# Layer 1's neighbour sums issued one slot at a time behind half products, and two blocks flipped through a diagonal

## The chip, the core and the metric

The kernel runs on one core of a Trainium2 chip. A core has five engines that each work through a queue of their own, in order: TensorE (PE, matrix products; its weight loads are listed as PEld), VectorE (DVE), ScalarE (ACT), GpSimd (POOL) and SyncE (SP). Transfers are issued from SP's and POOL's queues; the indirect ones, which gather or scatter rows by an index, all come from POOL. The metric is device time in microseconds (us) of one execution; lower is better.

## The reference

Two graph layers over 2708 nodes with 1024 features, all in float32. `adj` is a sparse 0/1 matrix; a few nodes have many neighbours, most have one to five, many none.

```python
def _L0_gnn_ref(sent_embed, adj_tensor, W_q, b_q, W_k, b_k, W_v, b_v):
    q, k, v = ...
    z = scale * (q @ k.T)
    spare_z = z * adj_tensor
    spare_z = jnp.where(spare_z == 0.0, -10000.0, spare_z)
    out = softmax(spare_z, axis=1) @ v
    return relu(out)
def _L1_gnn_ref(x, adj, weight, bias):
    return jnp.matmul(adj, jnp.matmul(x, weight)) + bias
x = _layernorm(x + _L0_gnn_ref(x, adj, ...))
x = _layernorm(x + _L1_gnn_ref(x, adj, ...))
```

Only layer 1 is touched by the change. Its result for one node is the normalised sum of the node's own row, the bias, and (sum of its neighbours' rows of x1) times the 1024x1024 weight, where x1 is layer 0's output.

## The kernel before

**Tiles.** The nodes are sorted by their number of neighbours into 22 blocks of up to 128 rows (P = 128). Block b has room for SLOTS[b] neighbours: 15, 11, 8, 6, 5, 4, 3 and 2 for blocks 0 to 7; 13, 5, 4, 4, 3, 3, 3, 2, 2, 2, 1 and 1 for blocks 8 to 19; blocks 20 and 21 have none. Blocks 18 and 19, which have one slot, are called `single`. The busiest rows are dealt out over several rows of block 0 and of a further block, "hub", with 11 slots and its sum in the tile `part`. `tabs` holds each row's neighbour indices, `valid` a 1 or 0 per slot. An index beyond the last row is left out by the gather, and `valid` then takes the slot's old contents out of the sum.

**Layer 1.** For each block, every slot is gathered from x1 in DRAM by an indirect transfer (`gather_slot`, line 483, POOL) into one of nine tiles named g, which are used in turn (`g_tile`), and added into the block's r by VectorE, times `valid` (line 1480). The first slot of most blocks is gathered straight into r; where not every row has a neighbour (block 0, hub, the single blocks and block 7), the first slot goes to a g tile and a pass of VectorE multiplies it by `valid` into r (line 1477). Then r is transposed ("flipped") on PE into rT: `flip` (line 953) makes eight transposes of 128x128 in two groups of four, ACT copies each group out of PSUM. Block 0's flip (`flip_shares`, line 966) is a matmul with a matrix of zeros and ones in the identity's place, which also folds in the hub's shares. Blocks are worked in pairs ("units"), in this order: (19, 18), (17, 16), (15, 1), (14, 2), (7, 8), (9, 3), (4, 10), (5, 11), (6, 0), (12, 13).

A unit's product is Strassen's scheme with seven half products (`pair_products`, line 311 through `half_products`), each of four matmuls of 128x128 by 128x512. It needs four sums of the halves of rT on VectorE (lines 1212 to 1215) and three differences of weight quarters besides a fourth made in place, t1 to t4 (lines 1537 to 1540, 128x2048 each), made once. Each half product's PSUM bank is emptied by one VectorE pass (line 333 or 1517, "eviction"), which has a high priority in the planner; several banks go on accumulating after an eviction, so a later half product of the unit waits for the eviction of an earlier one. The evictions add into xr, a gather of x1's own row onto a copy of the bias (line 467 on POOL, line 1490 on ACT). ACT normalises, POOL scatters the output rows (line 940).

**Order.** The program is emitted in the order of the Python code, and a planner moves instructions on each queue by priority and by when it thinks them ready. `follow(later, earlier)` adds a dependency; with same=True it only orders two instructions of the planner without a semaphore. In iteration i of the loop over units the sums of unit i+3 are emitted as a whole ahead of unit i's products; those of unit 2 stand in iteration 0, behind `halves_turned[-1]`, and the hub's in iteration 4. The list `began` holds the first matmul of every half product, and `between[n]` holds functions that are called while half product n is emitted, with its first matmul as argument; layer 0 uses it already.

**The seam.** Layer 0's last pair of blocks is normalised and scattered to x1 by a chain over VectorE (BN statistics line 1239, aggregate line 1019, four small passes), ACT and POOL; every gather of layer 1 waits for it. Meanwhile PE runs WARM = 13 matmuls whose result nobody reads (line 1530). The four quarters of the layer's weight are loaded by SP (line 1447) as soon as the last products on their buffers are done. The first difference t1 has a `follow` behind `firsts[0]`, the first mask pass of layer 1:

```python
follow(nc.vector.tensor_sub(t1, t1, w11), firsts[0], same=True)
nc.vector.tensor_sub(t2, w22, t1)
nc.vector.tensor_sub(t3, t2, w11)
nc.vector.tensor_sub(t4, w21, t2)
```

Of the kernel before, what the change touches and what calls it, by code (L numbers as in the profile page):

```python
# [9 lines left out]
F32 = mybir.dt.float32  # L10
# [6 lines left out]
ALU = mybir.AluOpType  # L17
# [4 lines left out]
P = 128  # L22
# [5 lines left out]
HUB_SLOTS = 11  # L28
HUB_KEYS = 80
RUN = 12  # L30
WARM = 13
FAMILY = 8


# [2 lines left out]
MIXED = [7]  # L37
# [7 lines left out]
RB = 5  # L45
# [39 lines left out]
def sparse_part(ctx, tc, x, xT, adj, wqT, wkT, wvT, bq, bk, bv, w1, b1, out):  # L85
    nc = tc.nc
    N, D = x.shape
# [11 lines left out]
    J0 = SLOTS[0]  # L99
    URGENT = 2000  # L100
    last = [b for b in range(NB) if SLOTS[b] == 0]
    single = [b for b in range(NB) if SLOTS[b] == 1]
# [11 lines left out]
    with es:  # L114
# [149 lines left out]
        def follow(later, earlier, same=False):  # L264

            kind = mybir.DependencyClass.NoSync if same else mybir.DependencyClass.Sync
            tc.add_manual_dep(later.ins, earlier.ins.name, mybir.DependencyInfo(kind, mybir.DependencyReason.DATA),
                              reason="an engine's queue shall not stand still for a transfer")
# [642 lines left out]
        def g_tile():  # L911

            filled[1] += 1
            return gp.tile([P, D], F32, name="g", tag=f"g{filled[1] % G1}", bufs=1)
# [31 lines left out]
        def flip(r, rT=None):  # L946

            rT = wp.tile([P, DC, P], F32, name="rT") if rT is None else rT
            for g in range(DC // 4):
                tr = p_tr.tile([P, 4, P], F32, name="tr")  # L950
                for k in range(4):
                    c = g * 4 + k
                    nc.tensor.transpose(tr[:, k, :], r[:, c * P:(c + 1) * P], ident)  # L953
                nc.scalar.copy(rT[:, g * 4:g * 4 + 4, :], tr)  # L954
            return rT

        def flip_shares(shares, rT=None):

            rT = wp.tile([P, DC, P], F32, name="rT") if rT is None else rT
            for g in range(DC // 4):  # L960
                tr = p_tr.tile([P, 4, P], F32, name="tr")
                for k in range(4):
                    c, at = g * 4 + k, 0
                    for r, to in shares:
                        n = to.shape[1]
                        nc.tensor.matmul(tr[:, k, at:at + n], r[:, c * P:(c + 1) * P], to, start=True, stop=True)
                        at += n
                nc.scalar.copy(rT[:, g * 4:g * 4 + 4, :], tr)
            return rT
# [231 lines left out]
        halves_turned = []  # L1201

        def turn_pair(flips, pool):

            A = []
            for k, flip_to in enumerate(flips):
                rT = pool.tile([P, DC, P], F32, name="rT", bufs=4)
                A.append(flip_to(rT))
            (a11, a12), (a21, a22) = [(a[:, :DC // 2], a[:, DC // 2:]) for a in A]
            s_all = wm_pool.tile([P, 4, DC // 2, P], F32, name="s_all", tag="m3")  # L1210
            S = [s_all[:, i] for i in range(4)]
            nc.vector.tensor_add(S[0], a21, a22)
            nc.vector.tensor_sub(S[1], S[0], a11)
            nc.vector.tensor_sub(S[2], a11, a21)
            halves_turned.append(nc.vector.tensor_sub(S[3], a12, S[1]))
            return A, S
# [243 lines left out]
        units = [(19, 18), (17, 16), (15, 1), (14, 2), (7, 8), (9, 3), (4, 10), (5, 11), (6, 0), (12, 13)]  # L1460
        assert sorted(last + [b for unit in units for b in unit]) == list(range(NB))
        last_norm = applied[-1]
        firsts = []

        def sum_rows(b, k=0, behind=None):
            if b == "hub":
                n, tab, ok, r = P, tab_h, valid_h, part
            else:
                n, tab, ok = (P, tab0, valid0) if b == 0 else (rows[b], tabs[:, b, :SLOTS[b]], valid[:, b, :SLOTS[b]])
                r = (cp if k else rp).tile([P, D], F32, name="r", bufs=3 if k else RB)  # L1470
            for j in range(tab.shape[1] if b else J0):
                if j == 0 and b not in [0, "hub"] + single + MIXED:
                    gather_slot(x1_d[:, :], tab[:n, 0:1], n, r)
                    continue
                xg = gather_slot(x1_d[:, :], tab[:n, j:j + 1], n, g_tile())
                if j == 0:
                    put = nc.vector.tensor_scalar(r[:n], xg[:n], ok[:n, 0:1], None, op0=ALU.mult)
                    firsts.append(put)
                else:
                    put = nc.vector.scalar_tensor_tensor(r[:n], xg[:n], ok[:n, j:j + 1], r[:n], op0=ALU.mult, op1=ALU.add)  # L1480
                if behind is not None:
                    follow(put, behind, same=True)
                    behind = None
            return r

        def gather_x1(b, k=0):

            n = rows[b]
            xr = (cp if k else wp).tile([P, D], F32, name="xr", bufs=2)
            follow(nc.scalar.copy(xr[:n], bias1[:n]), last_norm, same=True)  # L1490
            return gather_at(x1_d[:, :], tabs[:n, b, ROW:ROW + 1], n, xr, ALU.add)
# [12 lines left out]
            scatter(out, b, n, t, "out")  # L1504

        def turn1(unit, rs):
            return turn_pair([lambda rT, b=b, r=r: flip_shares([(part, to_h), (r, to_0)], rT) if b == 0 else flip(r, rT)
                              for b, r in zip(unit, rs)], cp)

        def work1(unit, A, S, xrs):  # L1510
# [20 lines left out]
            follow(put, products[-1], same=True)  # L1531

        got1, turned1, pending = {}, {}, []
        got1[0] = [sum_rows(b, k) for k, b in enumerate(units[0])]
        got1[1] = [sum_rows(b, k) for k, b in enumerate(units[1])]
        turned1[0] = turn1(units[0], got1.pop(0))
        follow(nc.vector.tensor_sub(t1, t1, w11), firsts[0], same=True)
        nc.vector.tensor_sub(t2, w22, t1)
        nc.vector.tensor_sub(t3, t2, w11)
        nc.vector.tensor_sub(t4, w21, t2)  # L1540
        xrs = {0: [gather_x1(b, k) for k, b in enumerate(units[0])]}
        for i, unit in enumerate(units):
            for p in pending:
                finish1(*p)
            if i + 1 < len(units):
                turned1[i + 1] = turn1(units[i + 1], got1.pop(i + 1))
                xrs[i + 1] = [gather_x1(b, k) for k, b in enumerate(units[i + 1])]
            if i == 0:
                got1[2] = [sum_rows(b, k, halves_turned[-1]) for k, b in enumerate(units[2])]
            if i + 3 < len(units):  # L1550
                got1[i + 3] = [sum_rows(b, k) for k, b in enumerate(units[i + 3])]
            if i == 4:
                sum_rows("hub")
            pending = list(zip(unit, *work1(unit, *turned1.pop(i), xrs.pop(i))))
            if i == len(units) - 4:
                some = test_scores()
            if i == len(units) - 2:
                raise_flag(some)
            if i in (4, 6):
                b = last[i // 2 - 2]  # L1560
                pending.append((b, gather_x1(b), None))
        for p in pending:
            finish1(*p)
        raised = nc.values_load(flag, min_val=0, max_val=1, skip_runtime_bounds_check_because="a comparison's result")
# [319 lines left out]
```

## Time and profile before

| | |
|---|---|
| median of 3 runs | 1009.27 us (1007.11, 1009.27, 1018.39) |
| the profiled execution | 1011.19 us, span 1009.5 us |
| PE busy over the span | 957.8 us (95%) |
| VectorE busy | 815.7 us (81%) |
| POOL busy (indirect transfers in layer 1) | 553.2 us (55%) |
| granted clock of TensorE, mean | 0.983 |
| layer 0's last half product ends | 697.24 us |
| first flip of layer 1 | 711.16 us |
| last half product of layer 1 ends | 995.83 us |

Times inside the execution are counted from the span's start. A line of the timeline gives the start, the length, the engine, the line of the kernel, the operation, what it writes and reads by the program's names, the shapes and the number of records; a matmul of 512 columns makes two records, a transpose one. In brackets stand the idle time of the engine ahead and what ended it. A busy PE isn't PE at full speed: the granted clock shows where the throttle had it slower.

### The profile page before, as it was taken

How to read it: one execution, taken by the hardware profiler on the slowest of the kernel's cores; microseconds unless marked ns; L12 is line 12 of the kernel's file. 1: busy time of each engine (PE TensorE's matmuls, PEld its weight loads, DVE VectorE, ACT ScalarE, POOL GpSimd, SP SyncE). 2: the span in 40 equal slices, each digit the busy share in tenths (PEclk: the TensorE clock that was granted, in tenths of full speed). 3: DMA queues.
4: the chain of work that ended last, by engine and by line, in shares of the span. 5: the costliest groups of instructions: out<-in, count | busy, mean ns of one | idle time of the engine just before them, and what ended most of it. 6: DMA issues, size and time to landing. Idle time of an engine off the chain costs nothing.

```text
span 1009.5 us, 10470 instructions
## 1 busy us (share of the span) xinstructions
PE 957.8 (95%) x2723; PEld 452.3 (45%) x2723; DVE 815.7 (81%) x1813; ACT 461.5 (46%) x1142; POOL 553.2 (55%) x443
## 2 busy tenths in 40 slices
PE   7989999999999999999899999999899899999994
PEld 6434444444444444454444444444444444435441
DVE  8999996995678896998899999984668977868532
ACT  4553466655543434233643544563242444252832
POOL 3841056133677574445466785621877878868420
PEclk9999999999999999999999999999999999989998
DMA  8475687769889676346537897756887699977631
GB/s 346 152 238 177 209 262 223 232 229 249 237 250 326 219 231 211 118 141 194 167 97 227 266 304 236 220 170 228 199 285 226 210 319 338 300 234 199 213 105 45
DMA packets 101342, 222.92 MB, mean 221 GB/s; under 512 B 19492, under 2 KB 46892, under 8 KB 101272
## 3 DMA queue, kind: packets, MB, share of 16 engines
q0 software_dynamic: 49424, 152.74, 49.8%
q1 hardware_dynamic: 51848, 69.41, 21.2%
q8 instruction: 23, 0.38, 0.1%
q14 instruction: 47, 0.39, 0.1%
HBM read 211.80 MB, written 33.64 MB: 243 GB/s over the span
## 4 chain that ended last, share of the span: by engine, by line
PE 52%; DVE 20%; issue 11%; DMA 7%; POOL 4%; ACT 4%; SPq 0%; POOLq 0%; DVEq 0%; ACTq 0%
PE po L311 29%; PE po L391 11%; PE tr L391 5%; PE tr L311 3%; DVE r L1097 3%; DVE junkv L1038 2%; DMA xr<-x_d,tabs 2%; DVE t L333 2%; DVE r L1480 2%; POOL wk_i L301 1%; POOL g L483 1%; DVE junkv L1294 1%; DVE at_a L242 1%; PE tr L953 1%; DMA g<-x_d,tabs 1%
## 5 line engine op out<-in xcount | busy, mean ns | idle before, releaser
L483 POOL DMA_INDIRECT g<-in_x_dram,tabs x84 | 112.6, 1341 | 81.9 <-DVE past_end L663 26.9
L311 PE MATMUL po<-t,s_all 128*128 128x512 f32 x320 | 146.2, 599 | 7.5 <-issue 3.8
L391 PE MATMUL po<-m,xt 128*128 128x512 f32 x288 | 124.8, 592 | 0.0
L1480 DVE SCALAR_TENSOR_TENSOR r<-g,valid,r 128x1024 f32<-128x1024 f32 x77 | 98.0, 1280 | 11.9 <-DMA g<-x_d,tabs 7.2
L311 PEld LDWEIGHTS po<-t,s_all 128*128 128x128 f32 x320 | 60.5, 191 | 85.8 <-issue 77.0
L483 POOL DMA_INDIRECT g<-x_d,tabs x66 | 77.4, 1172 | 26.0 <-issue 13.7
L1097 DVE SCALAR_TENSOR_TENSOR r<-g,pr,r 128x1024 f32<-128x1024 f32 x64 | 81.9, 1281 | 6.4 <-ACT r L1095 5.8
L1038 DVE SCALAR_TENSOR_TENSOR junkv<-yg,g 128x1024 uint8<-128x1024 f32 x69 | 84.4, 1224 | 2.6 <-DMA g<-in_x_dram,tabs 2.0
L391 PEld LDWEIGHTS po<-m,xt 128*128 128x128 f32 x288 | 54.6, 190 | 68.2 <-issue 67.4
L954 ACT COPY rT<-tr 128x512 f32<-128x512 f32 x76 | 41.6, 587 | 95.1 <-PE tr L953 93.5
L1000 ACT ACTIVATE junks<-t,lnm 128x1024 uint8<-128x1024 f32 (+1 forms) x40 | 45.8, 1144 | 84.6 <-DVE lnm L998 84.5
L242 DVE FIND_INDEX8 at_a<-ones,a 128x8 uint16<-128x234 f32 (+5 forms) x132 | 82.2, 627 | 0.0
L311 PE MATMUL po<-w,rT 128*128 128x512 f32 x160 | 75.2, 612 | 4.4 <-DVE t L1517 4.2
L256 ACT ACTIVATE junk<-a 128x2756 uint8<-128x2756 uint32 (+1 forms) x22 | 55.0, 2501 | 42.8 <-issue 15.8
L311 PE MATMUL po<-t,rT 128*128 128x512 f32 x160 | 73.7, 603 | 0.4 <-DVE t L1517 0.4
L311 PE MATMUL po<-wv,rT 128*128 128x512 f32 x160 | 73.5, 604 | 0.0
L311 PE MATMUL po<-w,s_all 128*128 128x512 f32 x160 | 73.4, 598 | 0.0
L311 PE MATMUL po<-wv,s_all 128*128 128x512 f32 x160 | 72.3, 592 | 0.0
L462 ACT ACTIVATE junka<-xt 128x128 f32<-128x128 f32 x168 | 51.7, 308 | 37.9 <-PE po L311 18.3
L1038 DVE SCALAR_TENSOR_TENSOR junkv<-xr,g 128x1024 uint8<-128x1024 f32 x37 | 45.4, 1226 | 19.1 <-DMA g<-in_x_dram,tabs 11.3
L940 POOL DMA_INDIRECT x_d<-t,tabs x22 | 27.7, 1257 | 51.3 <-ACT t L1014 17.6
L391 PE MATMUL tr<-m,xt 128*128 128x512 f32 x128 | 55.6, 592 | 0.0
(423 smaller groups left out, 1835.7 us busy)
## 6 DMA issues: line engine op xcount, KB each, us to landing
xt<-in_xT_dram SPq DMA_DIRECT2D x21, 512.0 KB
y_d<-yo SPq DMA_DIRECT2D x21, 512.0 KB
a<-in_adj_dram SPq DMA_DIRECT2D x21, 413.0 KB
a<-in_adj_dram SPq DMA_DIRECT2D x21, 338.0 KB
a<-in_adj_dram SPq DMA_DIRECT2D x21, 263.0 KB
wq_i<-in_wqT_dram SPq DMA_DIRECT2D x8, 512.0 KB
wk_i<-in_wkT_dram SPq DMA_DIRECT2D x8, 512.0 KB
wv<-in_wvT_dram SPq DMA_DIRECT2D x16, 256.0 KB
```

The costliest lines, as they stand in the source:

```text
L242: put = nc.vector.max_index(at[:n, i], ones[:n, :8], a[:n, cuts[i] + 8 * i:cuts[i + 1] + 8 * i + 8])
L256: put = nc.scalar.activation(junk[:n], loaded[b][:n, :AW].bitcast(U32), AF.Sign, accum_out=cnt[:n, b:b + 1])
L311: put = nc.tensor.matmul(acc, a[:, k], w[:, k], start=start and k == 0, stop=stop and k == DC // 2 - 1, skip_group_check=True)
L391: put = nc.tensor.matmul(po, xts[b][:, c, :], m_q[c // 4][h][:, c % 4], start=(c == 0), stop=(c == DC - 1))
L462: put = nc.scalar.activation(junka[:, :xt.shape[2]], xt[:, c, :], AF.Copy, accum_out=xs[:, c, b:b + 1])
L483: nc.gpsimd.indirect_dma_start(out=dst[:n], out_offset=None, in_=src, in_offset=bass.IndirectOffsetOnAxis(ap=at, axis=0), bounds_check=N - ...
L940: put = nc.gpsimd.indirect_dma_start(out=dst, out_offset=bass.IndirectOffsetOnAxis(ap=tabs[:n, b, ROW:ROW + 1], axis=0), in_=src[:n], in_o ...
L954: nc.scalar.copy(rT[:, g * 4:g * 4 + 4, :], tr)
L1000: nc.scalar.activation(junks[:n], t[:n], AF.Square, bias=nm[:n], accum_out=vs[:n])
L1038: put = nc.vector.scalar_tensor_tensor(junkv[:n], yg[:n], scale, xg[:n], op0=ALU.mult, op1=ALU.mult, accum_out=s)
L1097: nc.vector.scalar_tensor_tensor(r[:n], xg[j][:n], pr[:n, j:j + 1], r[:n], op0=ALU.mult, op1=ALU.add)
L1480: put = nc.vector.scalar_tensor_tensor(r[:n], xg[:n], ok[:n, j:j + 1], r[:n], op0=ALU.mult, op1=ALU.add)
```

## The change

Four things are edited.

1. `sum_rows` becomes `sums_of`, which returns the block's r and a list of functions, one for each slot. The loop hands them out by `some_sums` through `between`: in iteration 0 none behind half products one to three, then three, three, three and four; in every later iteration two behind each of the seven. Each VectorE pass of a slot follows the first matmul of the half product that it was emitted behind (now with a semaphore where one is needed). The order of blocks is units 2 to 6, the hub, units 7 to 9; what unit i+2 needs is emitted by the end of iteration i.
2. The single blocks 18 and 19 are gathered into a g tile that is itself their r, without the pass by `valid`. They are flipped by `flip_shares` with a diagonal matrix that holds `valid` (in the tiles far_h and far_0, which layer 0 no longer needs), so each flip is eight matmuls of 128x128 by 128x128 and no transposes. Two VectorE passes of 128x128 make the diagonals.
3. The differences t1 to t4 no longer follow a first mask pass, which for the single blocks there is no more.
4. WARM is 15 instead of 13.

```diff
-WARM = 13
+WARM = 15
...
-        firsts = []
-
-        def sum_rows(b, k=0, behind=None):
+
+        def sums_of(b, k=0):
...
-                r = (cp if k else rp).tile([P, D], F32, name="r", bufs=3 if k else RB)
-            for j in range(tab.shape[1] if b else J0):
-                if j == 0 and b not in [0, "hub"] + single + MIXED:
+                r = g_tile() if b in single else (cp if k else rp).tile([P, D], F32, name="r", bufs=3 if k else RB)
+
+            def slot(j, behind=None):
+                if j == 0 and b not in [0, "hub"] + MIXED:
                     gather_slot(x1_d[:, :], tab[:n, 0:1], n, r)
-                    continue
+                    return
...
                     put = nc.vector.tensor_scalar(r[:n], xg[:n], ok[:n, 0:1], None, op0=ALU.mult)
-                    firsts.append(put)
...
                 if behind is not None:
-                    follow(put, behind, same=True)
-                    behind = None
-            return r
+                    follow(put, behind)
+
+            return r, [lambda behind=None, j=j: slot(j, behind) for j in range(tab.shape[1] if b else J0)]
...
-            return turn_pair([lambda rT, b=b, r=r: flip_shares([(part, to_h), (r, to_0)], rT) if b == 0 else flip(r, rT)
+            return turn_pair([lambda rT, b=b, r=r: flip_shares([(part, to_h), (r, to_0)], rT) if b == 0 else
+                              flip_shares([(r, only[b])], rT) if b in only else flip(r, rT)
...
-        got1[0] = [sum_rows(b, k) for k, b in enumerate(units[0])]
-        got1[1] = [sum_rows(b, k) for k, b in enumerate(units[1])]
+
+        def begin_sums(u):
+            both = [sums_of(b, k) for k, b in enumerate(units[u])]
+            got1[u] = [r for r, _ in both]
+            return [slot for _, slots in both for slot in slots]
+
+        for b, to in zip(single, (far_h, far_0)):
+            nc.vector.tensor_scalar(to, ident, valid[:, b, 0:1], None, op0=ALU.mult)
+        only = dict(zip(single, (far_h, far_0)))
+        for u in range(2):
+            for slot in begin_sums(u):
+                slot()
         turned1[0] = turn1(units[0], got1.pop(0))
-        follow(nc.vector.tensor_sub(t1, t1, w11), firsts[0], same=True)
+        nc.vector.tensor_sub(t1, t1, w11)
...
+        to_sum, sums_left = list(range(2, 7)) + ["hub"] + list(range(7, len(units))), []
+
+        def some_sums(count, put):
+            for _ in range(count):
+                if not sums_left and to_sum:
+                    u = to_sum.pop(0)
+                    sums_left.extend(sums_of(u)[1] if u == "hub" else begin_sums(u))
+                if sums_left:
+                    sums_left.pop(0)(put)
+
...
-            if i == 0:
-                got1[2] = [sum_rows(b, k, halves_turned[-1]) for k, b in enumerate(units[2])]
-            if i + 3 < len(units):
-                got1[i + 3] = [sum_rows(b, k) for k, b in enumerate(units[i + 3])]
-            if i == 4:
-                sum_rows("hub")
+            at = len(began)
+            for k, count in enumerate((0, 0, 0, 3, 3, 3, 4) if i == 0 else (2,) * 7):
+                between[at + 1 + k] = [lambda put, count=count: some_sums(count, put)]
```

More of the change, by code (lines that the diff above doesn't have):

```diff
@@ L1561, in sparse_part @@
                 pending.append((b, gather_x1(b), None))
+        assert not to_sum and not sums_left
         for p in pending:
```

## The prediction

> **What bounds it now.** I read the page's slices first: PE is at 90% or more in nearly every slice, so only stretches in which PE stands or runs slowly can be won. The chain of waits for 660 to 1010 us says where: it follows PE to 697.24, leaves it for the last normalisation, the scatter of x1 and the first gather, and later hops between VectorE's sums, POOL and gathers. Then the timeline of PE from 690 us; the number before "PE" is the length, the bracket the idle time ahead and its releaser:
>
> ```profile
> 697.24 11.32 PE L1530 MATMUL tr<-y_bc,ident 128*128 128x512 f32 x26
> 711.16 1.07 PE L953 MATMUL tr<-ident,r 128*128 128x128 f32 x8 [2.60 <-DVE r L1477]
> 712.46 3.50 PE L311 MATMUL po<-w,rT 128*128 128x512 f32 x4 [0.24 <-ACT rT L954]
> ...
> 725.04 3.70 PE L311 MATMUL po<-t,s_all 128*128 128x512 f32 x8 [0.96 <-DVE xr L333]
> ...
> 752.26 3.70 PE L311 MATMUL po<-t,s_all 128*128 128x512 f32 x8 [2.04 <-issue]
> ...
> 885.58 2.07 PE L311 MATMUL po<-w,rT 128*128 128x512 f32 x2 [4.16 <-DVE t L1517]
> 887.45 5.01 PE L311 MATMUL po<-t,rT 128*128 128x512 f32 x8
> ```
>
> A matmul is two records, 0.858 us (a half product of four is 3.43 us). Seven half products and two flips are an undisturbed unit: 836.25 to 862.31, 26.06 us. What is lost after 725.04: the brackets 2.04, 1.44, 1.74, 0.42, 0.87, 4.16, 2.03 and 0.25 are 12.95 us; eight matmuls from 885.58 to 895.03 take 9.45 for 6.87 (2.58 lost), fourteen from 929.35 to 942.53 take 13.18 for 12.02 (1.16), and block 0's flip takes 3.92 where layer 0 took 3.10 (0.82). Together **17.5 us**, the most that better sums can give.
>
> VectorE's timeline at the seam of the layers:
>
> ```profile
> 694.01 0.69 DVE L333 TENSOR_TENSOR t<-po,t 128x512 f32<-128x512 f32 x1 [1.76 <-PE po L311]
> ...
> 697.44 0.69 DVE L333 TENSOR_TENSOR t<-po,t 128x512 f32<-128x512 f32 x1 [0.81 <-PE po L311]
> ...
> 699.63 0.21 DVE L1019 BATCH_NORM_AGGREGATE mv<-halves 128x2 f32<-128x12 f32 x1
> ...
> 710.26 0.75 DVE L1477 TENSOR_SCALAR r<-g,valid 128x1024 f32<-128x1024 f32 x1 [8.45 <-DMA g<-x_d,tabs]
> 710.93 2.28 DVE L1537 TENSOR_TENSOR w<-w,w 128x2048 f32<-128x2048 f32 x1
> ```
>
> VectorE has nothing to do from 701.8 to 710.26; the four weight differences (2.2 us each, back to back) begin after the first mask pass. And POOL, beside two of them:
>
> ```profile
> 710.05 1.08 POOL L483 DMA_INDIRECT r<-x_d,tabs  x1 [0.30 <-issue]
> 711.44 2.64 POOL L483 DMA_INDIRECT r<-x_d,tabs  x1 [0.30 <-issue]
> 714.38 2.56 POOL L483 DMA_INDIRECT g<-x_d,tabs  x1 [0.30 <-issue]
> ```
>
> **What the Trainium skill says.** "SBUF — State Buffer", Who interferes with whom: a tensor_tensor with both inputs in SBUF contends with GpSimd's reads; that it spares descriptor generation is marked there as inferred. The trace says otherwise: the four issues beside L1537 to L1540 take 2.64, 2.56, 3.13 and 2.49 us, against 0.99 for most, so I count 6.8 us of POOL time that they cost. "TensorE: Matmul & The Clock Gate", What's actually happening: PE drops to half clock after an idle window of about 3.4 us and needs as much activity to recover. It agrees: after the 2.60 us gap two matmuls take 3.50 instead of 1.72, and the granted clock is 0.50 from 714 to 716; after 4.16 us 2.58 us were lost. "DMA: Bandwidth & Descriptors", Anatomy of one DMA: 2 us plus bytes over 436 GB/s, for 0.5 MB an estimate of 3.2 us; the first gather takes 4.12 from issue to use, which I take.
>
> **The change, part by part.** The order of instructions in the built program of the changed kernel is known, and I lay the durations above on it.
>
> *The differences move up.* Without the follow to `firsts[0]`, they stand on VectorE inside layer 0's last evictions: the first after the fourth eviction, the second just ahead of the seventh, the third and fourth on both sides of the last BN statistics. The queue is in order, so the chain's own instructions wait. The third w1 load lands near 690.5 (DMA share 0.68 in that half microsecond, then 0.14), the fourth near 695.0 (0.89, then 0.07). So: first difference 690.7 to 692.9; evictions of the fifth and sixth product end about 695.7; t's sum pass to 696.4; second difference to 698.6; seventh eviction, one BN statistics and the sum pass 1.9; third difference 2.2, BN statistics 0.6, fourth difference 2.2: BN aggregate at 705.5, not 699.63. **+5.9 us** for the last normalisation, its scatter, and every gather: POOL's first gather is issued at 712.0 and is there at 716.1. ACT's chain and SP's loads are not moved. Nothing covers this. Two more warm matmuls (1.74 us) end at 710.3, inside the wait, and cost nothing; PE then stands 5.8 us, so I take the slow clock of the 4.16 us gap, 2.6.
>
> *No mask pass, a diagonal instead.* Gone: 0.92 us on the path (710.24 to 711.16) and two passes of 0.75 on VectorE. Added: two 128x128 passes in layer 0, nearest row 0.23 each; under 0.5 us, hidden by PE there, which has 20.0 of 20 us from 660 to 680. The 16 flips become real matmuls. No row has 128 columns: 96 take 0.28 and 32 take 0.17 apiece at full clock (489.17 to 492.27), on a line 0.335 for 128, so 5.4 us against 1.8 for transposes. From below the transposes' price (a gain of 3.6 on mine), from above a weight-bound 0.43 (1.5 more). First gather to third half product is then 5.4 + 16 transposes 1.8 + 8 matmuls 6.9 + 2.6 = 16.6, at 732.7; before, 14.8, at 725.04. **Head: +7.7 us.**
>
> *POOL at the head.* Without the differences beside it POOL regains 6.8 us, so unit 2's gathers come 0.9 us earlier than before, though it began 5.9 later, while PE comes 7.7 later: 8.6 us of new lead.
>
> *Sums singly behind half products.* No sum is added or saved (but the two masks); about two slots now follow each eviction, of blocks two units ahead, not three. The waits for PE are already met by the eviction ahead, so none is new. What stands behind a late gather are the evictions and, after them, PE. VectorE's load of a unit: about 12 sums of 1.22, seven evictions of 0.65, four additions of 0.61 and smalls, 22 of 26.06 us. POOL's: 14 gathers of 1.30 with gap, two xr of 1.87, two scatters of 1.35, 24.6 of 26.06. It fits, narrowly. Then the 6.5 us of gaps from 752 to 806 go, by POOL's lead; the hub's sums, now at most five in a row (6.1 us) between evictions two half products apart (6.87), no longer hold PE (4.16 and 2.58); and block 0's flips stand seven matmuls (6.0 us) later in PE's order, which covers 2.03 and its slow clock. Late next: gathers behind xr copies and output scatters in POOL's queue, which with two-unit lead I step through for units 1 to 3 and find VectorE waiting some 4 us for a gather, PE under 1 in each; I put 4 us of new stalls in all, bounds 0 and 25 (next part).
>
> Sum: +7.7 - 17.5 + 4 = **-5.8 us**. The profiled execution has 1011.19 us (span 1009.5), 1.9 over the median 1009.27; off the median the forecast is **1003.5 us**.
>
> **The rivals.**
> - *Nothing new stalls* (-9.8), or the diagonal flips also cost what transposes cost (-13.4). For it: POOL's and VectorE's loads are below 26 us. Against: both in-order queues at 85 to 95%. 996 to 999.5, about 997.
> - *The differences delay nothing*, as the head should be: gather at 710.24, PE warm until 710.3, third half product at 724.6; -17.9 + 4, so 995. Against it: the built order stands, and before's trace follows its own order.
> - *POOL becomes the bound, slower.* From 706.12 to 919.95 it made 130 issues in 213.8 us, 1.64 apart. If that interval stays, waits included, 18 issues are 29.6 us, 3.5 over a unit, in units 1 to 6: 21 us, PE stalled by in-order sums; -9.8 + 21 = +11, 1020. It turns the sign where the interval exceeds 1.54. Against it: 9 us of waits and the 6.8 us are in the 1.64; without them 1.52.
>
> **Numbers.** Forecast 0.55, its own range 999 to 1010; no new stalls 0.20; no delay 0.10; POOL bound 0.15. 1% is 10 us, about what a measurement tells from no change. Faster by more: the two quick cases but for their upper edge, 0.25, and a little of the forecast, 0.05, is 0.30; slower by more 0.12, most of the POOL case; within 0.58. The range 995 to 1016 leaves a tenth on either side, with the bounds of flips and stalls in it.
>
> **What shows it.** L1548 and its two followers ahead of the BN aggregate, and that at about 705.5; first diagonal flip near 716 after an idle PE of 5 to 6 us; third half product of unit 0 near 733; issues beside it at 1.0 us; no gap of 4 us near the hub. Wrong it would be if the aggregate stays at 699.6, if the 128-column flips take far from 0.34, or if PE shows gaps of over 2 us in each of units 1 to 6.

## The result, and the profile after

The changed kernel is slower: median 1022.64 us (20 runs, 1018.03 to 1029.82) against 1011.86 us for the kernel before (20 runs in all, 1006.71 to 1018.39). The ratio of the runs is **1.0115, 95% interval 1.0095 to 1.0134**. On the median that the prediction started from, 1009.27, this is 1020.9 us; 1003.5 was forecast, with 995 to 1016 as range.

The profiled execution took 1020.76 us, span 1019.0 (before 1011.19 and 1009.5). Two profiles of one kernel end layer 0 at times some microseconds apart, so I count layer 1 from the end of layer 0's last half product and cut it in two: the **head**, up to the end of unit 0's third half product, and the **body**, from there to the end of the last half product of all. Each kernel was profiled twice:

| | head | body | layer 1 |
|---|---|---|---|
| before | 27.8 and 27.9 us | 270.8 and 268.1 us | 298.6 and 296.1 us |
| after | 34.9 and 35.6 us | 277.9 and 277.1 us | 312.7 and 312.7 us |

So a profile can be read to about 2 or 3 us, and both parts got longer by more: 7 us in the head, 8 us in the body. PE's timeline after the change (start, length, operation, and in brackets the idle time ahead):

```profile
692.65 13.04 PE L1530 MATMUL tr<-y_bc,ident 128*128 128x512 f32 x30
712.94 3.75 PE L966 MATMUL tr<-far,g 128*128 128x128 f32 x16 [7.26 <-DMA g<-x_d,tabs]
716.49 2.58 PE L966 MATMUL tr<-far_h,g 128*128 128x128 f32 x16
...
727.52 3.60 PE L311 MATMUL po<-t,s_all 128*128 128x512 f32 x8
...
863.62 1.06 PE L953 MATMUL tr<-ident,r 128*128 128x128 f32 x8 [4.48 <-issue]
864.52 8.73 PE L311 MATMUL po<-w,rT 128*128 128x512 f32 x16
```

The warm matmuls start where layer 0 ends, and the first line with s_all ends the head: 727.52 - 692.65 = 34.87. Ahead of the first flip PE stands 7.26 us. In the body there are six gaps of 3.10, 3.18, 4.48, 2.34, 1.39 and 2.66 us, 17.15 in all, five of them ahead of flips; after the one shown, sixteen records take 8.73 us where they take 7.03 elsewhere. VectorE's timeline at the seam:

```profile
687.68 2.29 DVE L1547 TENSOR_TENSOR w<-w,w 128x2048 f32<-128x2048 f32 x1 [4.44 <-DMA w<-in_w_dram]
...
693.28 2.29 DVE L1548 TENSOR_TENSOR t<-w,w 128x2048 f32<-128x2048 f32 x1
...
697.28 2.29 DVE L1549 TENSOR_TENSOR t<-t,w 128x2048 f32<-128x2048 f32 x1
...
700.09 2.27 DVE L1550 TENSOR_TENSOR t<-w,t 128x2048 f32<-128x2048 f32 x1
702.28 0.20 DVE L1019 BATCH_NORM_AGGREGATE mv<-halves 128x2 f32<-128x12 f32 x1
```

All four differences stand ahead of the aggregate, which comes 9.63 us after layer 0's end instead of 2.39. The first of them even waits 4.44 us for its weights, with two evictions behind it. POOL's gathers at the head, in return, are quick now:

```profile
708.78 1.04 POOL L483 DMA_INDIRECT g<-x_d,tabs  x1 [2.61 <-DMA x_d<-t,tabs]
710.12 1.01 POOL L483 DMA_INDIRECT g<-x_d,tabs  x1 [0.30 <-issue]
```

In the body the trace shows a chain of waits. Its clearest case, from POOL's timeline and then VectorE's:

```profile
840.08 2.05 POOL L940 DMA_INDIRECT out_dram<-t,tabs  x1 [6.42 <-ACT t L1014]
...
848.02 1.02 POOL L483 DMA_INDIRECT r<-x_d,tabs  x1 [0.30 <-PE po L311]
849.34 0.99 POOL L483 DMA_INDIRECT g<-x_d,tabs  x1 [0.30 <-DMA xr<-x_d,tabs]
```
```profile
857.26 2.60 DVE L1479 SCALAR_TENSOR_TENSOR r<-g,valid,r 128x1024 f32<-128x1024 f32 x2 [5.12 <-DMA g<-x_d,tabs]
```

POOL stands 6.42 us at a scatter of output rows, because ACT has not normalised them; the gathers queued behind it go out that much later; VectorE waits 5.12 us for one; and the flip that needs the finished sum comes at 863.62, behind PE's gap of 4.48 us. Added up, POOL's waits in the 160 us after the head (what it waited for; us in total, times, longest), first before, then after:

```profile
POOL g L483 <- DVE r L1480: 5.7, 7, 2.3
...
POOL out_dram L940 <- issue: 2.7, 9, 0.3
```
```profile
POOL out_dram L940 <- ACT t L1014: 10.0, 4, 6.4
POOL xr L467 <- ACT xr L1489: 6.6, 5, 2.4
POOL out_dram L940 <- ACT xr L1014: 4.5, 1, 4.5
POOL out_dram L940 <- ACT rstd L1011: 3.6, 3, 2.9
```

Before, the scatters wait only the 0.3 us that lie between any two issues, and POOL now and then waits for a free tile, which means that it is ahead. After, it waits 18.1 us at scatters and 6.6 at xr gathers. In the second profiles ACT holds up the scatters for 0 us before and 19.0 after; at xr gathers it is 4.8 and 5.2, so those waits alone do not tell the two kernels apart. VectorE's sums stood 7.2 us for gathers over the whole kernel before, and 41.5 after (13.6 of it at the head):

```profile
L1480 DVE SCALAR_TENSOR_TENSOR r<-g,valid,r 128x1024 f32<-128x1024 f32 x77 | 98.0, 1280 | 11.9 <-DMA g<-x_d,tabs 7.2
```
```profile
L1479 DVE SCALAR_TENSOR_TENSOR r<-g,valid,r 128x1024 f32<-128x1024 f32 x77 | 98.6, 1282 | 44.4 <-DMA g<-x_d,tabs 41.5
```

### The profile page after: what moved, and what is told of

Same layout as the page of the kernel before. It is cut to its first block, busy times and chain, and to the rows that moved or that the text cites. A ratio compares the mean times of both kernels' runs of the same rounds, so it can differ in the third digit from the quotient of the medians.

```text
span 1019.0 us, 10482 instructions
## 1 busy us (share of the span) xinstructions
PE 962.8 (94%) x2743; PEld 458.7 (45%) x2743; DVE 813.7 (80%) x1813; ACT 465.2 (46%) x1142; POOL 548.5 (54%) x443
## 4 chain that ended last, share of the span: by engine, by line
PE 58%; DVE 15%; issue 9%; DMA 8%; ACT 4%; POOL 4%; SPq 0%; POOLq 0%; DVEq 0%; ACTq 0%
PE po L311 35%; PE po L391 11%; PE tr L391 5%; DMA g<-x_d,tabs 4%; PE tr L311 3%; DVE r L1097 2%; DVE junkv L1038 2%; PE tr L953 2%; DVE t L333 2%; DVE r L1479 1%; POOL wk_i L301 1%; ACT junks L1000 1%; DVE junkv L1294 1%; PE po L442 1%; DMA w<-in_w_dram 1%
## 5 line engine op out<-in xcount | busy, mean ns | idle before, releaser
L1479 DVE SCALAR_TENSOR_TENSOR r<-g,valid,r 128x1024 f32<-128x1024 f32 x77 | 98.6, 1282 | 44.4 <-DMA g<-x_d,tabs 41.5
L483 POOL DMA_INDIRECT g<-x_d,tabs x66 | 74.3, 1125 | 22.5 <-issue 14.7
L1000 ACT ACTIVATE junks<-t,lnm 128x1024 uint8<-128x1024 f32 (+1 forms) x40 | 45.9, 1147 | 83.0 <-DVE lnm L998 82.8
L311 PE MATMUL po<-w,s_all 128*128 128x512 f32 x160 | 75.6, 613 | 3.2 <-DVE r L1479 3.2
L954 ACT COPY rT<-tr 128x512 f32<-128x512 f32 x72 | 39.5, 589 | 67.7 <-PE tr L953 60.2
L462 ACT ACTIVATE junka<-xt 128x128 f32<-128x128 f32 x168 | 52.0, 310 | 33.0 <-PE po L311 14.2
L1489 ACT COPY xr<-bias 128x1024 f32<-128x1024 f32 (+1 forms) x22 | 22.8, 1046 | 89.1 <-DVE t L1517 71.7
L1038 DVE SCALAR_TENSOR_TENSOR junkv<-xr,g 128x1024 uint8<-128x1024 f32 x37 | 45.4, 1226 | 17.0 <-DMA g<-in_x_dram,tabs 11.6
```

The lines of the kernel that those rows point to most:

```text
L311: put = nc.tensor.matmul(acc, a[:, k], w[:, k], start=start and k == 0, stop=stop and k == DC // 2 - 1, skip_group_check=True)
L462: put = nc.scalar.activation(junka[:, :xt.shape[2]], xt[:, c, :], AF.Copy, accum_out=xs[:, c, b:b + 1])
L483: nc.gpsimd.indirect_dma_start(out=dst[:n], out_offset=None, in_=src, in_offset=bass.IndirectOffsetOnAxis(ap=at, axis=0), bounds_check=N - ...
L1000: nc.scalar.activation(junks[:n], t[:n], AF.Square, bias=nm[:n], accum_out=vs[:n])
L1038: put = nc.vector.scalar_tensor_tensor(junkv[:n], yg[:n], scale, xg[:n], op0=ALU.mult, op1=ALU.mult, accum_out=s)
```

## The experiments

For the body there were three theories. **Theory 1**: the sums now run two units ahead, not three, and POOL's in-order queue then reaches scatters and xr gathers before what they wait for is done. **Theory 2**: single sums, each tied to its half product, starve VectorE. **Theory 3**: POOL's issue rate is the bound, whatever the order. For the head, the hoisted differences stand against the diagonal flips.

All ratios are to the kernel before on the same chip, with 95% intervals. "POOL" is the sum of POOL's waits of over 0.35 us in the 160 us after the head, whatever ended them. The expectations that start from 34.7 or 34.5 us for the change, where the table has 24.1, also count two waits inside the head: 7.95 us ahead of layer 0's last scatter of x1 and 2.61 ahead of the first gather.

| kernel | units ahead, sums | head | body | POOL | ratio |
|---|---|---|---|---|---|
| before | 3, whole | 27.8 | 270.8 | 4.8 | 1 |
| after | 2, single | 34.9 | 277.9 | 24.1 | 1.0115 (1.0095 to 1.0134) |
| a_late | 2, single | 30.0 | 276.6 | 20.7 | 1.0106 (1.0081 to 1.0132) |
| a_whole | 3, whole | 34.7 | 265.8 | 8.5 | 1.0050 (1.0021 to 1.0078) |
| a_three | 3 slots at a time | 35.3 | 291.8 | 9.7 | 1.0302 (1.0270 to 1.0333) |
| a_later | 2, single | 35.2 | 282.5 | 23.3 | 1.0158 (1.0116 to 1.0201) |
| a_ahead | 3, single | 33.5 | 264.5 | 7.1 | 1.0012 (0.9993 to 1.0031) |
| a_whole2 | 2, whole | 35.2 | 280.9 | 23.7 | 1.0224 (1.0196 to 1.0253) |
| a_untied | 2, single | 35.4 | 277.7 | 23.4 | 1.0144 (1.0115 to 1.0172) |
| b_diag | 3, whole | 30.1 | 264.7 | 8.3 | 1.0016 (0.9995 to 1.0037) |
| a_const | 2, single | 42.0 | 269.0 | 24.0 | 1.0149 (1.0110 to 1.0188) |
| c_best | 3, single | 31.6 | 264.0 | 9.3 | 0.9993 (0.9967 to 1.0019) |
| a_const2 | 2, single | 33.9 | 264.2 | 8.3 | 0.9998 (0.9967 to 1.0029) |
| c_best2 | 3, single | 26.8 | 273.9 | 4.4 | 0.9982 (0.9959 to 1.0005) |
| a_split | 2, single | 34.9 | 263.7 | 14.4 | 1.0038 (1.0018 to 1.0058) |
| a_split_late | 2, single | 30.1 | 264.6 | 12.7 | 0.9955 (0.9929 to 0.9980) |

### The head and the sums, taken apart

a_late is the change with its differences behind the last VectorE operation of layer 0's last normalisation (`tails` holds it):

```diff
-        nc.vector.tensor_sub(t1, t1, w11)
+        follow(nc.vector.tensor_sub(t1, t1, w11), tails[0], same=True)
```

> The changed kernel with one thing undone: the four weight differences follow the last VectorE operation of layer 0's last normalisation again. Layer 1 is measured from the end of layer 0's last half product to the end of its own last (before 298.6 us, changed 312.7); the head is the part up to the end of unit 0's third half product (27.8 and 34.9). Theory 1 (gathers stand in POOL's queue behind xr gathers and output scatters that wait, because sums are only two units ahead): head back to 28 to 29, the part after it stays near 278 or grows by 1 to 4, since the differences lie beside gathers again; layer 1 306 to 311, ratio to the kernel before 1.004 to 1.009. Theory 2 (the tie of each sum to a half product starves VectorE): the same head, 278 after it. Theory 3 (POOL's issue rate is the bound): the head's gain is given back in full, layer 1 312 to 314, ratio 1.011. If the prediction's head term is wrong and the diagonal flips, not the differences, cost it, the head stays at 33 or more.

Head 30.0 instead of 34.9 us, body 276.6: the hoisted differences cost the head 4.8 us. PE's timeline shows where the other 2.2 us over the kernel before lie:

```profile
695.81 13.04 PE L1530 MATMUL tr<-y_bc,ident 128*128 128x512 f32 x30
711.80 3.51 PE L966 MATMUL tr<-far,g 128*128 128x128 f32 x16 [2.95 <-DMA g<-x_d,tabs]
...
725.84 3.60 PE L311 MATMUL po<-t,s_all 128*128 128x512 f32 x8
```

From the first flip to the end of the head it is 14.0 us, where the kernel before took 13.9 (711.16 to 725.04), so the diagonal flips cost nothing here that can be seen; the first flip itself comes 2.1 us later after layer 0's end, for a reason that c_best's lines show below. The head is longer than expected (28 to 29), and the time fell by less than expected (1.004 to 1.009): 1.0106 against 1.0115, which is 0.9 us and uncertain by some 3.

a_whole has the head of the change and the sums of the kernel before:

```diff
-WARM = 13
+WARM = 15
...
-                r = (cp if k else rp).tile([P, D], F32, name="r", bufs=3 if k else RB)
+                r = g_tile() if b in single else (cp if k else rp).tile([P, D], F32, name="r", bufs=3 if k else RB)
...
-        follow(nc.vector.tensor_sub(t1, t1, w11), firsts[0], same=True)
+        nc.vector.tensor_sub(t1, t1, w11)
```

The diagonals of the change, its edit 2, are in it too.

> The kernel before with the hoisted differences, the diagonal flips, no mask pass and 15 warm matmuls of the change, but sums in whole blocks three units ahead as before. All theories: head 34 to 36 us. Theories 1 and 2: the part after the head 266 to 272 us as in the kernel before (270.8) or a little less, as POOL's issues are quick at the head; layer 1 301 to 307, ratio 1.003 to 1.008. Theory 3 (POOL's rate, the same instructions here as in the change): part after the head 276 to 279, ratio 1.010 to 1.013. VectorE's waits for gathers at the sums: 5 to 12 us in theories 1 and 2, over 30 in theory 3.

Head 34.7, body 265.8, POOL's waits 8.5 us instead of 24.1: with the very instructions of the change POOL keeps pace, so **theory 3 falls**. What the change costs in the body lies in the order of the sums.

### Two attempts that told little

a_three tried to gain lead with more slots at a time:

```diff
-            for k, count in enumerate((0, 0, 0, 3, 3, 3, 4) if i == 0 else (2,) * 7):
+            for k, count in enumerate((0, 0, 0, 3, 3, 3, 4) if i == 0 else (3,) * 7):
```

> The changed kernel with three sums behind each half product from unit 1 on instead of two, so that the sums run further ahead, up to what their buffers hold. Theory 1 (lead): VectorE's waits for gathers fall from 41.5 us to under 20, PE's gaps after the head from 17 us to under 9, layer 1 from 312.7 to 302 to 307, ratio to before 0.999 to 1.006. Theory 2 (tie): no gain or a loss, since three tied sums stand between evictions; 312 to 318. Theory 3 (issue rate): 311 to 314, waits as in the change.

It is slower by 3%, for a reason of its own. VectorE's and PE's timelines:

```profile
905.00 13.17 DVE L1479 SCALAR_TENSOR_TENSOR r<-g,valid,r 128x1024 f32<-128x1024 f32 x10
```
```profile
918.83 2.08 PE L311 MATMUL po<-w,rT 128*128 128x512 f32 x2 [18.63 <-DVE t L1517]
```

The planner set ten sums in a row ahead of an eviction, and PE stood 18.63 us. That says nothing on lead.

a_later moved a unit's norms and scatters behind the next unit's half products 1 and 2, and the xr gathers behind 3 and 4:

```diff
-            for p in pending:
-                finish1(*p)
...
+                for k, b in enumerate(units[i + 1]):
+                    between[at + 3 + k] = [lambda put, i=i, k=k, b=b: xrs[i + 1].append(gather_x1(b, k))] + between[at + 3 + k]
+            for k, p in enumerate(done):
+                between[at + 1 + k] = [lambda put, p=p: finish1(*p)] + between[at + 1 + k]
```

> The changed kernel with the norms and output scatters of a unit and the xr gathers of the next one put behind its half products 1 to 4, where what they wait for is done, instead of ahead of the unit. Theory 1 (waiting instructions in POOL's queue): POOL's waits for ACT in layer 1 fall from some 20 us to under 8, VectorE's waits for gathers from 41.5 to under 20, PE's gaps after the head from 17 to under 9, layer 1 302 to 307, ratio to before 0.999 to 1.006. Theories 2 and 3: POOL's waits fall but layer 1 stays at 311 to 315.

POOL's waits stayed at 23.3 us, now all of them at scatters: norm and scatter had moved together, so a scatter still met a norm that was not done. The wait it was to take away was not taken away.

### Lead or form: the four corners

a_ahead keeps single, tied sums but emits unit i+3's in iteration i, as before (what these lines replace is left out here); a_whole2 is a_whole with unit i+2's, and the hub's in iteration 5:

```diff
+            if i == 0:
+                for k, slot in enumerate(begin_sums(2)):
+                    slot(halves_turned[-1] if k == 0 else None)
+            slots = (begin_sums(i + 3) if i + 3 < len(units) else []) + (sums_of("hub")[1] if i == 4 else [])
+            for k in range(7):
+                now = slots[k * len(slots) // 7:(k + 1) * len(slots) // 7]
+                between[at + 1 + k] = [lambda put, now=now: some_sums(now, put)]
```
```diff
-            if i + 3 < len(units):
-                got1[i + 3] = [sum_rows(b, k) for k, b in enumerate(units[i + 3])]
...
+            if i + 2 < len(units):
+                got1[i + 2] = [sum_rows(b, k, halves_turned[-1] if k + i == 0 else None) for k, b in enumerate(units[i + 2])]
```

> The changed kernel with sums still taken singly and tied to half products, but three units ahead as in the kernel before: unit 2's in one block behind the first flips, then unit i+3's spread over unit i's seven half products. Theory L (what costs is the lead, two units instead of three): the part of layer 1 after the head (265.8 us with whole blocks three ahead, 277.9 in the change) is 264 to 270, VectorE's waits for gathers there 8 to 15 us instead of 30, ratio to the kernel before 1.002 to 1.008. Theory 2 (the single sums and their ties starve VectorE): 275 to 280 us, ratio 1.010 to 1.014. Head 34 to 36 in both.

> Whole blocks, untied, with the head of the change, but only two units ahead: the other corner. Theory L: the part after the head 274 to 281 us, VectorE's waits for gathers 22 to 35 us, ratio to the kernel before 1.009 to 1.014. Theory 2: 264 to 270 us, waits 8 to 15, ratio 1.003 to 1.007.

a_untied hands the slots no half product to follow:

```diff
-                between[at + 1 + k] = [lambda put, count=count: some_sums(count, put)]
+                between[at + 1 + k] = [lambda put, count=count: some_sums(count, None)]
```

> The changed kernel with the ties taken away: the sums stand in the program where they stood, but none waits for its half product. Theory L: part after the head 275 to 280 us, ratio 1.010 to 1.013, no difference to the change that can be measured. Theory 2: 264 to 270, ratio 1.002 to 1.007.

The bodies fall into two pairs. Three units ahead: 265.8 (whole) and 264.5 (single). Two: 280.9 (whole, POOL waiting chiefly at xr gathers, 16.2 us) and 277.9 (single; 277.7 untied). **The lead decides, not the form**, and theory 2 falls. One size missed: a_whole2's ratio of 1.0224 and its VectorE waits for gathers, 45.9 us in the body, lie above what was expected (1.009 to 1.014, 22 to 35 us); why its time is so long wasn't followed up. a_ahead's waits in POOL's queue, in the 160 us after its head:

```profile
POOL xr L467 <- ACT xr L1489: 7.1, 1, 7.1
...
POOL out_dram L940 <- issue: 2.7, 9, 0.3
```

Ahead of the scatters stands no more than the usual 0.3 us: with a third unit's gathers ahead of them in the queue, ACT is done when their turn comes.

b_diag puts the diagonal and the late differences of a_late into the kernel before.

> The kernel before (whole blocks three units ahead) with single blocks gathered without a mask pass and flipped with the diagonal, and the differences behind the last normalisation's last VectorE operation. Head 29 to 31 us, as with the differences there in the changed kernel (30.0). Theory L: part after the head 265 to 271, ratio to the kernel before 0.998 to 1.004. Theory 2 makes the same forecast here; if the differences beside the first gathers cost POOL its lead, 270 to 274 and 1.003 to 1.007.

Head 30.1, as expected, body 264.7, just under the range; the time is not measurably other than before.

### Which wait it is

A scatter from a tile that is long ready takes the wait away and leaves the scatter (the kernel then leaves out those output rows):

```diff
-            scatter(out, b, n, t, "out")
+            scatter(out, b, n, bias1 if any(b in unit for unit in units[:6]) else t, "out")
```

> The changed kernel with one wait taken away: the output scatters of units 0 to 5 write a constant tile that is long ready instead of t, so POOL issues as many scatters of the same size at the same places in its queue but need not wait for ACT's normalisation (the output of those rows is left out; the norms are still computed). If POOL's waits in its queue are what makes gathers late with two units of lead: POOL's waits in the 160 us after the head fall from 34.7 us to 12 to 22, the part of layer 1 after the head from 277.9 us to 268 to 274, ratio to the kernel before 1.002 to 1.009. If the lead itself matters and not what POOL waits for (POOL would stand without work either way, waiting for buffers): waits on other releasers take their place, 275 to 280 us, 1.010 to 1.014.

Nothing held these scatters back any more, so the planner put eight ahead of the first gathers. PE's first flip came late, and the head took 42.0 us:

```profile
725.34 3.75 PE L966 MATMUL tr<-far,g 128*128 128x128 f32 x16 [13.86 <-DMA g<-x_d,tabs]
```

The body, 269.0, had lost scatters as well as waits. In a_const2 they stay in the body by waiting for a half product that is done (again these output rows are left out):

```diff
+            early = any(b in unit for unit in units[:6])
+            put = scatter(out, b, n, bias1 if early else t, "out")
+            if early:
+                follow(put, began[-6])
```

> The changed kernel with the output scatters of units 0 to 5 reading a constant tile and waiting for the second half product of their unit, which is long done, instead of for ACT's norm (those rows of the output are left out). They stay behind their unit in POOL's queue. If the scatters' waits are the cause: POOL's waits in the 160 us after the head 34.5 us in the changed kernel, here 12 to 22; the part after the head 266 to 273 us instead of 277.5; ratio to the kernel before 1.000 to 1.008. If POOL stands for lack of work either way: waits for xr or for free tiles take the scatters' place, 28 us or more in the 160 us; 275 to 280 us; ratio 1.010 to 1.014. Head 34 to 36 in both.

Body 264.2 instead of 277.5, ratio 0.9998. POOL's waits in the 160 us:

```profile
POOL out_dram L940 <- ACT xr L1014: 6.4, 1, 6.4
...
POOL out_dram L940 <- issue: 2.8, 9, 0.3
```

One wait is left, at a scatter that was not edited. With as many issues as in the change and two units of lead, the loss is gone. Two things went with the wait, as POOL's timeline shows at the place that was shown of the change:

```profile
831.76 1.03 POOL L940 DMA_INDIRECT out_dram<-bias,tabs  x1 [0.30 <-issue]
833.10 0.96 POOL L940 DMA_INDIRECT out_dram<-bias,tabs  x1 [0.31 <-issue]
834.36 2.20 POOL L467 DMA_INDIRECT xr<-x_d,tabs  x1 [0.30 <-issue]
...
839.37 1.04 POOL L483 DMA_INDIRECT r<-x_d,tabs  x1 [0.30 <-issue]
```

Both scatters now go out ahead of both xr gathers, where the change had one behind them, and the waits at xr gathers fell too (0.5 us instead of 6.6). Is it the scatters' wait, then, and does a kernel that computes everything do as well? a_split leaves the norms where they are and emits the two scatters behind the third and fourth half products of the next unit:

```diff
-            scatter(out, b, n, t, "out")
+            if at is None:
+                scatter(out, b, n, t, "out")
+            else:
+                between.setdefault(at, []).append(lambda put: scatter(out, b, n, t, "out"))
...
-            for p in pending:
-                finish1(*p)
+            for k, p in enumerate(pending):
+                finish1(*p, len(began) + 3 + k)
...
+                between.setdefault(at + 1 + k, []).append(lambda put, count=count: some_sums(count, put))
```

> The changed kernel, everything computed, with the output scatters alone put later in POOL's queue: a unit's norms stay where they are, its two scatters are issued behind the third and fourth half products of the next unit, after several gathers and with the norm long done. If the scatters' wait for the norm, with too few gathers ahead of it, is the cause: POOL's waits in the 160 us after the head fall from 34.5 us to 8 to 20, the part after the head from 277.5 to 264 to 270 us, layer 1 298 to 304, ratio to the kernel before 1.000 to 1.006. If it isn't: 274 to 280 us, 1.009 to 1.014.

Body 263.7. POOL's waits, and its timeline and PE's at the place that was shown of the change:

```profile
POOL xr L467 <- ACT xr L1489: 11.3, 5, 4.8
POOL out_dram L940 <- issue: 2.7, 9, 0.3
...
POOL out_dram L940 <- ACT rstd L1011: 2.1, 1, 2.1
```
```profile
848.75 1.02 POOL L940 DMA_INDIRECT out_dram<-t,tabs  x1 [0.30 <-DMA xr<-x_d,tabs]
...
852.69 1.02 POOL L940 DMA_INDIRECT out_dram<-t,tabs  x1 [0.30 <-issue]
```
```profile
862.40 1.93 PE L953 MATMUL tr<-ident,r 128*128 128x128 f32 x16
864.17 7.03 PE L311 MATMUL po<-w,rT 128*128 128x512 f32 x16
```

The scatters go out without waiting, with four gathers of the next sums ahead of the first, and PE runs through its flips without a gap. POOL's waits for ACT at scatters fell from 18.1 to 2.1 us, and those at xr gathers rose from 6.6 to 11.3, without bringing the loss back. Here the scatters stand later in the queue, in a_const2 earlier, and the body is 264 us in both: what the two share is that the scatters no longer wait, so **the scatters' wait for the norm is the cause** of the change's loss in the body. The sum of POOL's waits fell less than expected (24.1 to 14.4; 24.9 on the expectation's count, not 8 to 20). So that sum alone doesn't tell the loss; which gathers stand behind the wait does.

> The same with the differences behind the last normalisation's last VectorE operation. Head 29.5 to 31.5 us instead of 34 to 36, part after the head 264 to 271, ratio to the kernel before 0.996 to 1.003; it beats the kernel before only if the part after the head is below 266.

With the late differences of a_late as well, **0.9955 (0.9929 to 0.9980)**: this kernel beats both, by 0.45% and, ratio against ratio, by 1.6%. Against a_split, 1.0038, the late differences bring 8 us in the time, against 0.9 for a_late over the change and 3.9 of layer 1 in the profiles; how much of the head comes out in the time isn't settled closer than that.

### What the head still costs

c_best is a_ahead with late differences and a mask in place of the diagonal, on the single blocks' own tile:

```diff
+                    if b in single:
+                        nc.vector.tensor_scalar(r[:n], r[:n], ok[:n, 0:1], None, op0=ALU.mult)
```

> Single sums three units ahead, the differences behind the last normalisation, and single blocks gathered without a second tile but masked in place on VectorE and flipped by transposes as before. Head 28 to 29.5 us (27.8 in the kernel before, 30.0 to 30.1 with the diagonal and late differences), part after the head 264 to 267, layer 1 292 to 296; ratio to the kernel before 0.993 to 1.001.

The body came as expected, the head was 31.6. POOL's timeline shows why:

```profile
703.91 2.28 POOL L940 DMA_INDIRECT x_d<-t,tabs  x1 [4.62 <-ACT t L1031]
708.81 2.12 POOL L483 DMA_INDIRECT g<-x_d,tabs  x1 [2.61 <-DMA x_d<-t,tabs]
711.23 1.88 POOL L483 DMA_INDIRECT g<-x_d,tabs  x1 [0.30 <-issue]
```

The differences now run beside the scatter of x1 and the first two gathers, and each issue takes some 1 us longer. In a_late these three take as long (2.28, 2.12 and 1.86 us), which fits its late first flip. c_best2 lets them follow the first mask pass again.

> As c_best, but the differences begin after the first mask pass again, as in the kernel before. If they cost c_best's head by standing beside the scatter of x1 and the first two gathers: the scatter 0.95 us instead of 2.28, the first gathers 1.0 instead of 2.12 and 1.88, the head 27.5 to 28.5 instead of 31.6. Part after the head 264 to 267 if single sums three ahead do as well as before, layer 1 292 to 295; ratio to the kernel before 0.993 to 0.999. If the differences there cost POOL its lead: part after the head 268 to 271, ratio 0.997 to 1.002.

POOL's timeline at the same place:

```profile
702.17 0.95 POOL L940 DMA_INDIRECT x_d<-t,tabs  x1 [4.62 <-ACT t L1031]
705.72 1.03 POOL L483 DMA_INDIRECT g<-x_d,tabs  x1 [2.60 <-DMA x_d<-t,tabs]
```

Head 26.8, the shortest of all, and body 273.9, longer than either range that was expected. In part the differences now cost later: four of POOL's issues beside them take 1.90, 3.15, 2.98 and 2.50 us, VectorE then waits 4.50 us for a gather, and PE's gaps in the first 40 us of the body are 5.1 us instead of 1.4 in c_best. The rest of the 9.9 us isn't accounted for. The time, 0.9982, can't be told from the kernel before.

before_again and after_again are the second profiles in the table at the top.

> The kernel before once more, for a second profile: layer 1 within 3 us of 298.6, the part after the head within 3 us of 270.8; more than that says how far one profile can be read.

> The changed kernel once more, for a second profile: layer 1 within 3 us of 312.7, the part after the head within 3 us of 277.9, head 34 to 36.

Both hold.

## Why the prediction was wrong

**The step that failed** is the body's, -17.5 + 4. It forecast 253.3 us of work without a stall (270.8 - 17.5) and "4 us of new stalls in all"; the body measured 277.9, so **24.6 us** of stall stand where 4 were forecast: 17.15 of gaps, the rest mostly the slow matmuls behind them. The four corners divide the 24.6. With the lead kept the body is 264.5 to 265.8, so 11 to 13 us are stalls that do not go even then, and cutting the lead adds the other 12 to 13. Both terms were mis-sized:

- **The new stalls**, 4 us forecast, 12 to 13 shown. The mechanism was named word for word, "gathers behind xr copies and output scatters in POOL's queue, which with two-unit lead I step through"; but stepping through three units and finding "PE under 1 in each" sized it at a third. "It fits, narrowly" was where to stop: 24.6 of 26.06 us leaves POOL 1.46 us a unit, and no wait was charged against it. The trace after has 13 waits for ACT of 24.7 us in 160 us, 20.8 beyond the usual gaps, which is 3.4 us a unit of 26.06: 1.9 more than there is, 12 us over 6.1 units, as an estimate. The agreement is rough: the same working would give a_split, whose waits at xr gathers remain, a loss of some 3 us that it doesn't show. Without the scatters' waits a_split is 14.2 us quicker in the body.
- **The stalls that were to go**, 17.5 us forecast. With three units and the change's head the gain is 2 to 6 us on the two profiles before. PE's gaps of 8 to 11 us stay in both, at evictions and flips.

**The head** came out at +7.1 us (+7.7 in the second pair), with +7.7 forecast; the mechanism was right, but that the sum agrees so closely is luck, as its terms erred both ways. The aggregate was at 9.63 us after layer 0's end where 705.5 meant 8.3: the first difference, held up by its weights, began 5.0 us ahead of layer 0's end, not 6.5. The sixteen diagonal matmuls, priced at 5.4 us and 2.6 for a slow clock, took 5.96 us with the slow clock in it (712.94 to 718.90). a_late shows that hoisting the differences is what the head pays for: 4.8 us of the 7. Behind the norm they aren't free either: in c_best they add 3.3 us to three of POOL's issues. **POOL at the head** regained its time as forecast (the first gathers' issues at 0.99 to 1.04 us, not 2.5).

**The rivals.** "POOL becomes the bound" gave 1020, and 1020.9 it was, by its own reading: an issue interval that stays as it is, "waits included". Counted from the first gather to the end of block 0's last, it was 1.67 us before (128 issues in 213.8 us; the prediction took 130, and so 1.64) and 1.70 after (132 in 224.7). Against it I held that 9 us of waits would fall out of it; they rose to over 20. The issues themselves are no bound: a_const2 makes them all, 1.60 us apart, and its body is 264.2. The two quick rivals had no part in it. Of the tests that it named, "gaps of over 2 us in each of units 1 to 6" came true for units 1, 3, 5 and 6.

**A reading.** The prediction calls the slow clock after a gap of 2.60 us an agreement with an idle window of about 3.4. The gap is shorter than that, so the line does not bear the figure out. The price taken from the trace held: 2.6 us forecast, 2.4 lost here (5.96 us for sixteen matmuls of 0.22).

Left open: layer 1 grew by 15.4 us in the mean of two profiles, the time by 1.15%, some 11.6 us; over all kernels of the table the two differ by up to some 5 us. Where layer 0 ends doesn't explain it: 692.65 and 694.94 in the profiles after lie among the 692.65 to 699.50 of all 18, and with the same head a_untied ends it at 699.50 and a_three at 698.53.

## What to carry to other kernels

A lead in an in-order queue does more than bring data early: it gives other instructions in that queue time until what they wait for is done. Before a lead is cut, list what in the queue waits for the work now running, here output scatters behind a norm, and hold each wait against the queue's slack per unit (a warning, not a price: which gathers stand behind the wait decides); if it doesn't fit, move the waiting instruction behind later gathers, which here was worth as much to the body as the third unit of lead (263.7 and 264.5 us). And an instruction that is freed of an order falls where its inputs come ready, which can be in the middle of the chain that the next stage waits for.

## What the hardware showed unexpectedly

- A float32 matmul of 128x128 by 128 columns takes 0.22 us at full clock (eight in 1.78 us, 719.62 to 721.40 in the second profile after), twice the 0.11 us of a transpose; the line through 96 and 32 columns had given 0.335. It is even less than the 0.28 us of 96 columns in those rows, where matmuls of 96 and 32 columns alternate, so they did not give the price of columns alone; the cause wasn't tried.
- The scatter of x1 beside a VectorE tensor_tensor of 128x2048 took 2.28 us to issue, alone 0.95; so a scatter is slowed as gathers are (2.12 against 1.03). The Trainium skill, "SBUF — State Buffer", Who interferes with whom, infers that such an operation spares GpSimd's descriptor generation; these lines say otherwise again.
